# Local attention and a routed feed-forward layer on one core: row turns in steps apart, projection parts halved, layernorm and routing moved between GpSimd's folds, and the third routing table one block later

## The chip, the cores and the metric

The kernel runs on one core of one Trainium2 chip. The metric is the device time of one execution in microseconds (us). Five engines work side by side, each through its own instructions in the order in which the program gives them: TensorE (PE in the profile; its weight loads are PEld), VectorE (DVE), ScalarE (ACT), GpSimd (POOL) and SyncE (SP), which only issues DMAs. An instruction waits on semaphores for what it needs, and everything behind it on its engine waits with it.

## The reference

The input x is (2, 2048, 256) in f32. Two post-layernorm sublayers are computed:

```python
# causal local attention, 16 heads of 16, each row sees itself and the 64 before it
q, k, v = split(x @ W_attn + b_attn)
a = softmax(mask(q @ k.T / 4)) @ v
x1 = layernorm(x + a @ W_proj + b_proj)
# routed feed-forward: 8 experts, each token goes to the one with the largest logit
e = argmax(x1 @ Wr.T)
y = gelu(x1 @ W1[e] + b1[e]) @ Wo + bo + x1
out = layernorm(x1 + layernorm(y) * gamma + beta)
```

## The kernel before

**Attention loop.** The 4096 rows are 32 tiles of 128 and 8 chunks of 4 tiles. One loop of 32 steps handles four tiles at once, at different stages. In step i, tile t = i gets its scores (L513, L525, into four PSUM banks r = 0 to 3), its negated row maxima (`row_max`, L537, VectorE) and its exps (`exps`, L541, ScalarE, four per bank). GpSimd adds the exps up (`fold`, L553 after banks 0 and 1 and again after banks 2 and 3, then three halvings, L561). Tile u = i - 1 has its four banks of probabilities turned (`turn`, L591) and copied from PSUM (`keep_turned`: banks 0 and 2 by ScalarE, L597; 1 and 3 by VectorE, L599), and is weighed with v (`weigh`, L611). Tile w = i - 2 gets its sums inverted (`inverse`, L569, L574), spread by GpSimd (rw, L577), turned (`turn_inverse`, L630) and multiplied in (`normalise`, L634); then the output projection and the statistics for the layernorm (`join`, L642 to L652). Tile z = i - 3 gets the power of its variance on GpSimd (`norm_scale`, rs, L658 and L659), its layernorm x1 on VectorE (`norm`, L667) with a store of x1 to DRAM by SP (L670), and is turned for the router (`turn_x1`, L680; `keep_x1`, L685). Every fourth step computes router logits for four tiles (`route`, L692), turned one step later (`turn_logits`, L702).

**Projection parts.** Each chunk of x needs eight parts. Piece 0 turns the rows of x (`project`, L403, four short transposes per part); pieces 1 and 2 make q and k (L407, two 512-wide matmuls per part); piece 3 makes v (L414, four 256-wide matmuls per part). Each goes through a PSUM tile of a pool of two that `weigh` shares, and `keep` copies it out. A step has two slots for parts: slot 0 before the turns of banks 2 and 3, slot 1 behind them. Up to step 23 two parts run per step in plain order, so both parts of piece 0 fall into one step (3, 7, 11, and so on); steps 24 to 29 have one part each, in slot 1. `add_bias` (L1087, GpSimd) adds the bias to a chunk's residual at the end of a step.

**Routing.** Each token's expert, and its place among the tokens of that expert, is found by small VectorE operations, written as generators (`hot`, `places`, `first_blocks`, `other_blocks`, `rest_blocks`) that `some(task, n)` advances by n operations and `rest(task)` finishes. A dictionary `plan` gives them to the ends of steps. A table of the tokens of each block (`table`, L922) is a product of one-hot rows (`one_hots`, L827; `late_one_hots`, L833) and marks, accumulated by TensorE over all tiles. The first table is made in step 30; the second and third later.

**Blocks.** After the loop, 25 full blocks of 128 tokens of one expert each (`block(b)`) gather their tokens by an indirect DMA of GpSimd (L143), turn them (L181), run the first layer (L215) and the GELU (L226), and the second layer (L235); `finish_block` ends with two layernorms on VectorE and GpSimd (L245 to L265) and an indirect store (L267). The first layer of block b + 1 runs ahead of the second layer of block b. The remaining 7 x 128 tokens are taken in "late" blocks that the third table lists; 11 further first layers run over parts of these tokens, spread over the last full blocks (`firsts`), and seven second layers close the kernel. Dictionary `beside` gives the routing work to places (b, 0) to (b, 2) of the blocks; the third table stands at (13, 0), ahead of block 14's first layer, its rows in blocks 10 to 12 on VectorE (3 and 5 per block) and GpSimd (3, 3 and 2).

The order of every engine is the order of the calls: the whole is recorded under a manual schedule.

Of the kernel before, what the change touches and what calls it, by code (L numbers as in the profile page):

```python
# [33 lines left out]
def kernel(  # L34
# [90 lines left out]
    f6 = ctx.enter_context(tc.tile_pool(name="f6", bufs=5))  # L125
# [152 lines left out]
    with ExitStack() as att:  # L278
# [67 lines left out]
        off_i = aw.tile([P, P], I32, name="off_i")  # L346
        lag_i = aw.tile([P, 2, CTX], I32, name="lag_i")
# [50 lines left out]
        def project(c, piece, part):  # L398

            pm = psum(f"pj_{c}_{piece}_{part}")  # L400
            if piece == 0:
                for j in range(TPC):
                    nc.tensor.transpose(pm[:, ts(j, P)], xts[c][:, j, ts(part, P)], ident)  # L403
            elif piece in (1, 2):
                f = (piece - 1) * KC + part
                for k in range(KC):
                    nc.tensor.matmul(  # L407
                        pm, lhsT=wa[:, k, ts(f, P)], rhs=axT[c][:, k, :],
                        start=(k == 0), stop=(k == KC - 1),
                    )  # L410
            else:
                for a in range(2):
                    for k in range(KC):
                        nc.tensor.matmul(  # L414
                            pm[:, ts(a, C)],
                            lhsT=axT[c][:, k, ts(2 * part + a, P)],
                            rhs=wa[:, k, 2 * C : 3 * C],
                            start=(k == 0), stop=(k == KC - 1),
                        )
            pxs[c, piece, part] = pm  # L420

        def prepare(c, piece):

            first = c % (TPB // TPC) == 0
            if piece == 0:
                if c + 1 < B * T // CH:
                    xts[c + 1] = load_x(c + 1)
                axT[c] = p2.tile([P, KC, CH], F32, tag="xT", name=f"xT_{c}", bufs=1)
                xbs[c] = xp.tile([P, TPC, C], F32, tag="xb", name=f"xb_{c}")
            elif piece == 1:  # L430
                qs[c] = p2.tile([P, KC, 2, CH], F32, tag="q", name=f"q_{c}")
            elif piece == 2:
                ks[c] = p2.tile([P, KC, CTX + CH], F32, tag="k", name=f"k_{c}")
                if first:
                    nc.gpsimd.memset(ks[c][:, :, 0:CTX], 0.0)
                else:
                    nc.gpsimd.tensor_copy(ks[c][:, :, 0:CTX], ks[c - 1][:, :, CH : CH + CTX])
            else:

                vs[c] = p2.tile([P, TPC, NH // 2, 3, HD], F32, tag="v", name=f"v_{c}")  # L440
                nc.gpsimd.memset(vs[c][:, :, :, 1, :].rearrange("p j m d -> p (j m) d"), 0.0)

                vh[c] = p2.tile([P, TPC, NH // 2, 3, HD], F32, tag="h", name=f"h_{c}")
                if first:
                    nc.gpsimd.memset(vh[c][0:CTX, 0].rearrange("p m s d -> p (m s d)"), 0.0)

        def keep(c, piece, part):
# [31 lines left out]
            else:  # L479
                for a in range(2):  # L480
                    nc.vector.tensor_tensor(
                        vs[c][:, 2 * part + a, :, 0::2, :],
                        pm[:, ts(a, C)].rearrange("p (m s d) -> p m s d", s=2, d=HD),
                        bv_bc.rearrange("p (m s d) -> p m s d", s=2, d=HD),
                        ALU.add,
                    )
                v, h = vs[c], vh[c]
# [78 lines left out]
        def inverse(i):  # L566

            sm = small.tile([P, NH], F32, tag="sm", name=f"sm_{i}")
            nc.vector.tensor_reduce(sm, sums.pop(i)[:, :, 0:8], AX.X, ALU.add)  # L569
            spread_inverse(i, sm)  # L570

        def spread_inverse(i, sm):
            ri = small.tile([P, NH], F32, tag="ri", name=f"ri_{i}")
            nc.vector.reciprocal(ri, sm)  # L574
            rw = p2.tile([P, KC, 4, 2, HD], F32, tag="rw", name=f"rw_{i}")
# [86 lines left out]
        def norm(i):  # L662
# [3 lines left out]
            x1 = xp.tile([P, C], F32, tag="x1", name=f"x1_{i}", bufs=3)  # L666
# [20 lines left out]
        def route(c):  # L687
# [8 lines left out]
            lT = p2.tile([P, P], F32, tag="lT", name=f"lT_{c}")  # L696
# [19 lines left out]
        def iota(shape, pattern, base, cm, name):  # L716
            ti = rt.tile(shape, I32, name=f"{name}_i")
# [367 lines left out]
        def add_bias(c, tiles=TPC, first=0):  # L1085
            some = slice(first, first + tiles)
# [4 lines left out]

        for n in range(3):
# [7 lines left out]
        def quick_sums(i, r):  # L1100
# [4 lines left out]
            if r == 3:  # L1105
                spread_inverse(i, sums.pop(i))
# [3 lines left out]
        parts = [(c, n, p) for c in range(1, NT // TPC) for n in range(TPC) for p in range(2)]  # L1110
        work, at = {0: parts[:4]}, 4
        for i in range(1, NT - 2):
            count = 2 if i < NT - TPC - 4 else 1
            work[i] = parts[at : at + count]
            at += count
        assert at == len(parts)


        plan, spread, running = {}, {}, {}
# [15 lines left out]
        def put(at, *call):  # L1135
            plan.setdefault(at, []).append(partial(*call))


        for n, (t0, t1) in enumerate(lots[:EARLY]):
            at = t1 + 4  # L1140
            put(at, some, ("hot", n), 3)
            put(at + 1, rest, ("hot", n))
            put(at + 2, rank, n)
            put(at + 2, some, ("places", n), 1)
            put(at + 3, some, ("places", n), 3)
            put(at + 4, rest, ("places", n))
            for t in range(t0, t1, 2):
                spread[at + 5 + (t - t0) // 2] = [partial(one_hots, nc.gpsimd, t)]
        at = SPLIT[EARLY] + 6
        for n in range(7):  # L1150
            put(at + n, some, "first", 1 if n < 3 else 3)
        put(at + 7, rest, "first")
        put(at + 8, table, 0)
# [4 lines left out]
        for i in range(NT):  # L1158
# [3 lines left out]
            todo = work.get(i, [])  # L1162
            slots = [None] * (2 - len(todo)) + todo
            for part in todo:
                if part[2] == 0 and i > 0:
                    prepare(*part[:2])
# [4 lines left out]
            if i == 0:  # L1171
# [7 lines left out]
                for part in [(0, 3, 0), (0, 3, 1)] + todo[:2]:  # L1179
                    project(*part)  # L1180
                    keep(*part)
                add_bias(0)
                for r in range(2, 4):
                    exps(t, r)
                for part in todo[2:]:
# [7 lines left out]
            if u is not None:  # L1193
                turn(u, 0)
                keep_turned(u, 0)
                turn(u, 1)
            exps(t, 0)
# [3 lines left out]
            if z is not None:  # L1201
                norm_scale(z)
# [4 lines left out]
            row_max(t, 3)  # L1207
# [9 lines left out]
            if slots[0]:  # L1217
                keep(*slots[0])
            if z is not None:
                norm(z)  # L1220
            exps(t, 2)
            if slots[1]:
                project(*slots[1])
# [3 lines left out]
            if t == NT - 1:  # L1227
                for b in range(2):
                    gather(b)
                inverse(u)  # L1230
                quick_sums(t, 0)
            if slots[1]:
                keep(*slots[1])
# [23 lines left out]
            if i >= NT - TPC:  # L1257
                add_bias(i // TPC, 1, i % TPC)
            elif todo[-1:] and todo[-1][1:] == (3, 1):
                add_bias(todo[-1][0])  # L1260
# [84 lines left out]
    begin = 2 * NFULL - main + 1  # L1345
    for b in range(begin, NFULL):
        firsts[b].append(b - begin + NFULL)
    firsts[NFULL - 1].append(main - 1)
# [8 lines left out]
    def block(b):  # L1357
# [61 lines left out]
        (13, 0): [partial(table, 2)],  # L1419
# [5 lines left out]
    for b in range(10, 13):  # L1425
# [3 lines left out]
        beside[b, 2] = [partial(late_one_hots, nc.gpsimd, 3 * b - 6, min(3 * b - 3, NT))]  # L1429
# [76 lines left out]
```

## Time and profile before

| What | us |
|---|---|
| median of 3 runs (lowest, highest) | 604.82 (604.8, 605.92) |
| the profiled execution | 605.1 |
| its span, first to last instruction | 603.3 |
| first scores (step 0) start at | 14.86 |
| step 4 starts at | 51.83 |
| step 24 starts at | 245.08 |
| step 31 starts at | 311.54 |
| first second layer (block 0) starts at | 339.29 |
| second layer of block 12 starts at | 428.96 |
| last second layer (the 32nd) starts at | 585.56 |

The page divides the span into 40 slices of 15.1 us. Steps take from 8.0 to 12.6 us and full blocks 7.25 us where nothing else is in them, so two slices hold about three steps or four blocks. A matmul's end is modelled, so a busy TensorE in the profile is one with work in its pipeline. "ph", "py", "pj", "pt", "pa", "pr", "px", "pl" are PSUM tiles of the first layer, second layer or output projection, parts, turned probabilities, weighed values, turned inverse, turned x1 and logits.

### The profile page before, as it was taken

How to read it: one execution, taken by the hardware profiler on the slowest of the kernel's cores; microseconds unless marked ns; L12 is line 12 of the kernel's file. 1: busy time of each engine (PE TensorE's matmuls, PEld its weight loads, DVE VectorE, ACT ScalarE, POOL GpSimd, SP SyncE). 2: the span in 40 equal slices, each digit the busy share in tenths (PEclk: the TensorE clock that was granted, in tenths of full speed). 3: DMA queues.
4: the chain of work that ended last, by engine and by line, in shares of the span. 5: the costliest groups of instructions: out<-in, count | busy, mean ns of one | idle time of the engine just before them, and what ended most of it. 6: DMA issues, size and time to landing. Idle time of an engine off the chain costs nothing.

```text
span 603.3 us, 18546 instructions
## 1 busy us (share of the span) xinstructions
PE 560.2 (93%) x7311; PEld 455.8 (76%) x7312; DVE 406.6 (67%) x958; ACT 301.8 (50%) x1005; POOL 413.5 (69%) x613
## 2 busy tenths in 40 slices
PE   8999999999999999998978999999789999999990
PEld 5676766766767667666756898999689999999980
DVE  5668778789798788989976567887633323324482
ACT  2568666675657665675655433233224554554200
POOL 5367776776768868687873388888868766633473
PEclk9999999999999999999989999999989999999996
DMA  5311430210301202001423455555537677573010
GB/s 157 90 48 51 119 100 11 60 59 21 92 20 32 86 26 57 21 20 46 111 84 117 158 176 171 173 176 184 166 106 237 198 246 249 173 242 130 18 38 26
DMA packets 35605, 64.79 MB, mean 107 GB/s; under 512 B 8558, under 2 KB 23484, under 8 KB 35516
## 3 DMA queue, kind: packets, MB, share of 16 engines
q1 hardware_dynamic: 32444, 55.19, 29.3%
q0 software_dynamic: 3072, 8.39, 4.3%
q8 instruction: 59, 0.97, 0.7%
q14 instruction: 30, 0.25, 0.1%
HBM read 48.93 MB, written 8.39 MB: 95 GB/s over the span
## 4 chain that ended last, share of the span: by engine, by line
PE 66%; POOL 14%; DVE 9%; ACT 6%; issue 4%; DMA 0%; POOLq 0%; DVEq 0%; ACTq 0%
PE ph L215 14%; PE py L235 11%; PE pj L407 9%; PE pt L591 6%; PE pa L611 5%; PE s L525 5%; PE py L642 4%; PE pj L414 4%; ACT pr L541 4%; PE s L513 2%; POOL out_dram L267 2%; POOL xg L143 2%; DVE nm L537 2%; PE px L680 2%; POOL row L827 1%
## 5 line engine op out<-in xcount | busy, mean ns | idle before, releaser
L541 ACT ACTIVATE pr<-s,nm 128x128 f32<-128x128 f32 x512 | 140.9, 412 | 7.9 <-DVE nm L537 7.9
L553 POOL TENSOR_TENSOR fd<-pr 128x512 f32<-128x512 f32 x62 | 78.7, 1270 | 72.8 <-ACT pr L541 71.9
L226 ACT ACTIVATE gT<-ph,bc 128x128 f32<-128x128 f32 x200 | 57.0, 368 | 118.5 <-issue 63.0
L215 PE MATMUL ph<-xgT,wb 128*128 128x128 f32 x800 | 96.5, 279 | 0.0
L215 PEld LDWEIGHTS ph<-xgT,wb 128*128 128x128 f32 x800 | 95.3, 195 | 1.5 <-issue 0.2
L235 PE MATMUL py<-wo_sb,gT 128*128 128x256 f32 x400 | 90.6, 380 | 0.0
L537 DVE TENSOR_REDUCE nm<-s 128x4 f32<-128x512 f32 x128 | 81.6, 679 | 7.0 <-PE s L525 6.7
L561 POOL TENSOR_TENSOR fd<-fd 128x512 f32<-128x512 f32 (+2 forms) x93 | 76.4, 822 | 7.3
L235 PEld LDWEIGHTS py<-wo_sb,gT 128*128 128x128 f32 x400 | 74.1, 190 | 9.0
L597 ACT COPY pT<-pt 128x512 f32<-128x512 f32 x64 | 38.4, 601 | 82.6 <-DVE nm L537 27.9
L591 PE MATMUL pt<-ident,pr 128*128 128x128 f32 x512 | 71.8, 280 | 6.8 <-DVE pT L599 3.5
L591 PEld LDWEIGHTS pt<-ident,pr 128*128 128x128 f32 x512 | 55.9, 141 | 24.2 <-issue 10.6
L407 PE MATMUL pj<-xT,wa 128*128 128x512 f32 x128 | 60.1, 595 | 0.8 <-ACT xT L451 0.8
L255 DVE TENSOR_TENSOR y<-py,xbo 128x256 f32<-128x256 f32 x32 | 13.5, 422 | 57.7 <-PE py L235 54.3
L599 DVE COPY pT<-pt 128x512 f32<-128x512 f32 x64 | 43.7, 683 | 10.3 <-PE pt L591 10.2
L525 PEld LDWEIGHTS s<-k,q 32*64 32x64 f32 x2048 | 30.9, 130 | 13.6 <-issue 13.6
L215 PE MATMUL ph<-xpT,wb 128*128 128x128 f32 x352 | 40.9, 275 | 0.0
L215 PEld LDWEIGHTS ph<-xpT,wb 128*128 128x128 f32 x352 | 40.2, 192 | 0.1
L525 PE MATMUL s<-k,q 32*64 32x128 f32 x2048 | 38.6, 278 | 0.0
L642 PE MATMUL py<-wpj,av 128*128 128x256 f32 x128 | 34.2, 390 | 2.8 <-DVE logits L703 2.0
L265 DVE TENSOR_SCALAR res<-y,mv_c,rs_c 128x256 f32<-128x256 f32 x32 | 15.9, 498 | 30.5 <-POOL rs_c L249 30.4
L407 PEld LDWEIGHTS pj<-xT,wa 128*128 128x128 f32 x128 | 22.0, 190 | 18.9 <-issue 15.8
(236 smaller groups left out, 988.4 us busy)
## 6 DMA issues: line engine op xcount, KB each, us to landing
wb<-in_L_ffn_W_dram SPq DMA_DIRECT2D x33, 1024.0 KB, 5.2
h<-v SPq DMA_DIRECT2D x24, 192.0 KB, 3.8
xt<-in_L_attn_x_dram SPq DMA_DIRECT2D x8, 512.0 KB, 3.8
x_d<-x SPq DMA_DIRECT2D x32, 128.0 KB, 2.8
wb<-in_L_ffn_W_dram SPq DMA_DIRECT2D x24, 128.0 KB, 2.8
h<-v SPq DMA_DIRECT2D x14, 96.0 KB, 2.6
wo_sb<-in_L_ffn_Wo_dram SPq DMA_DIRECT2D x1, 1024.0 KB
wa<-in_L_attn_W_attn_dram SPq DMA_DIRECT2D x3, 256.0 KB, 5.8
```

The lines of the kernel that those rows point to most:

```text
L215: nc.tensor.matmul(phs[b, h][:, f % (NF // 2), :], lhsT=wb[:, k, ts(f, P)], rhs=xT[:, k, :], start=(k == 0), stop=(k == KC - 1),)
L226: nc.scalar.activation(gT[:, f, :], ph[:, f % (NF // 2), :], AF.Gelu, bias=bcs[b][:, f : f + 1], scale=1.0,)
L235: nc.tensor.matmul(py[:, 0:C], lhsT=gT[:, f, :], rhs=wo_sb[:, f, :], start=(f == 0), stop=(f == NF - 1),)
L407: nc.tensor.matmul(pm, lhsT=wa[:, k, ts(f, P)], rhs=axT[c][:, k, :], start=(k == 0), stop=(k == KC - 1),)
L525: nc.tensor.matmul(banks[i][r][a * CTX : (a + 1) * CTX, 2 * g + o, :], lhsT=qs[c][rows, g, o, t0 : t0 + CTX], rhs=ks[c][rows, g, t0 : t0 + P],
L537: nc.vector.tensor_reduce(maxes[i][:, r, :], banks[i][r], AX.X, ALU.max, negate=True)
L541: nc.scalar.activation(probs[i][:, r, x, :], banks[i][r][:, x, :], AF.Exp, bias=maxes[i][:, r, x : x + 1], scale=1.0,)
L553: nc.gpsimd.tensor_tensor(fd[:, 8 * pair : 8 * pair + 8, :], pr[:, two, :, 0:CTX].rearrange("p r x c -> p (r x) c"), pr[:, two, :, CTX:P]. ...
L561: nc.gpsimd.tensor_tensor(fd[:, :, 0:n], fd[:, :, 0:n], fd[:, :, n : 2 * n], ALU.add)
L591: nc.tensor.transpose(pt[:, x, :], probs[i][:, r, x, :], ident)
L599: nc.vector.tensor_copy(pTs[i][:, r], pt)
L642: nc.tensor.matmul(py[:, 0:C], lhsT=av[:, k, :], rhs=wpj[:, k, :], start=(k == 0), stop=(k == KC - 1),)
```

## The change

The work done stays the same except for its order; buffers change where the order needs it.

- Slots: `project` and `keep` take `halves`, so that a part may be done in two halves. The two turns of a chunk's rows now stand in slot 0 of two even steps, two steps apart (step 4m + 2 for chunk m + 2 and step 4m + 4), each with one whole matmul part in slot 1; odd steps have two whole matmul parts. From step 25 to 28, and in step 3, one part is halved over slots 0 and 1; the last part is halved over slot 1 of steps 29 and 30.
- In a step, GpSimd first makes rs (`norm_scale`), then rw (`spread_inverse`, split from `inverse`), then what `prepare` needs, then one half of `add_bias`, and only then the folds. `norm` moves up on VectorE, to behind the second copy of a turned bank and ahead of the row maxima of banks 2 and 3.
- Most routing operations move from the end of a step to behind `normalise` (`early`), those of the first table one step earlier at the end.
- Loads of x are issued with `add_bias` instead of with piece 0.
- Blocks: the third table moves to (14, 0); its rows are all made by VectorE in blocks 10 to 13. The 11 further first layers begin one block later (block 16) and the last two full blocks take two each.
- Buffers: xT 1 to 2, x1 3 to 2, lT 2 to 1, gathered tokens xg 5 to 4; some integer temporaries share other tiles.

```diff
-    f6 = ctx.enter_context(tc.tile_pool(name="f6", bufs=5))
+    f6 = ctx.enter_context(tc.tile_pool(name="f6", bufs=4))
...
-        def project(c, piece, part):
+        def project(c, piece, part, halves=(0, 1)):
-            pm = psum(f"pj_{c}_{piece}_{part}")
+            if (c, piece, part) not in pxs:
+                pxs[c, piece, part] = psum(f"pj_{c}_{piece}_{part}")
+            pm = pxs[c, piece, part]
...
-                for k in range(KC):
+                for k in halves:
...
-                if c + 1 < B * T // CH:
-                    xts[c + 1] = load_x(c + 1)
-                axT[c] = p2.tile([P, KC, CH], F32, tag="xT", name=f"xT_{c}", bufs=1)
-                xbs[c] = xp.tile([P, TPC, C], F32, tag="xb", name=f"xb_{c}")
+                axT[c] = p2.tile([P, KC, CH], F32, tag="xT", name=f"xT_{c}")
...
-            x1 = xp.tile([P, C], F32, tag="x1", name=f"x1_{i}", bufs=3)
+            x1 = xp.tile([P, C], F32, tag="x1", name=f"x1_{i}")
...
-        parts = [(c, n, p) for c in range(1, NT // TPC) for n in range(TPC) for p in range(2)]
-        work, at = {0: parts[:4]}, 4
-        for i in range(1, NT - 2):
-            count = 2 if i < NT - TPC - 4 else 1
-            work[i] = parts[at : at + count]
-            at += count
+        parts = [(c, n, p) for c in range(1, NT // TPC) for n in range(1, TPC) for p in range(2)]
+        line = iter(parts[2:])
...
+        work = {i: [None, None] for i in range(NT)}
+        for i in range(1, NT - 1):
+            c = i // TPC + (1 if i % TPC == 0 else 2)
+            if i % 2 == 0 and c < NT // TPC:
+                work[i] = [(c, 0, 0 if i % TPC else 1, (0, 1)), whole()]
+            elif i == 3 or NT - 7 <= i < NT - 3:
+                one = next(line)
+                work[i] = [one + ((0,),), one + ((1,),)]
+            elif i == NT - 3:
+                one = next(line)
+                work[i][1], work[i + 1][1] = one + ((0,), True), one + ((1,), True)
+            elif i < NT - 3:
+                work[i] = [whole(), whole()]
...
-        at = SPLIT[EARLY] + 6
-        for n in range(7):
-            put(at + n, some, "first", 1 if n < 3 else 3)
-        put(at + 7, rest, "first")
-        put(at + 8, table, 0)
+        at = SPLIT[EARLY] + 7
+        for n in range(6):
+            put(at + n, some, "first", 3 if n < 5 else 2, to=early)
+        put(at + 6, rest, "first", to=early)
+        put(at + 7, table, 0)
...
+            if z is not None:
+                norm_scale(z)
+            if w is not None:
+                spread_inverse(w)
...
+            if i >= TPC - 1 and i % TPC in (0, TPC - 1):
+                c = (i + 1) // TPC
+                if c < NT // TPC:
+                    add_bias(c, 2, 2 if i % TPC == 0 else 0)
+                if i % TPC == 0 and c + 2 < NT // TPC:
+                    xts[c + 2] = load_x(c + 2)
             exps(t, 0)
             row_max(t, 1)
             if u is not None:
                 keep_turned(u, 1)
             if z is not None:
-                norm_scale(z)
+                norm(z)
             if slots[0]:
                 project(*slots[0])
             exps(t, 1)
             row_max(t, 2)
-            row_max(t, 3)
+            if slots[0]:
+                row_max(t, 3)
             if t < NT - 1:
                 fold(t, 0)
...
-            if z is not None:
-                norm(z)
             exps(t, 2)
             if slots[1]:
-                project(*slots[1])
+                project(*slots[1][:4])
             if w is not None:
                 turn_inverse(w)
                 normalise(w)
...
+            for task in early.get(i, ()):
+                task()
...
-    begin = 2 * NFULL - main + 1
+    begin = 2 * NFULL - main + 2
...
-        (13, 0): [partial(table, 2)],
+        (14, 0): [partial(table, 2)],
...
-    for b in range(10, 13):
+    for b in range(10, 14):
         at = 8 * (b - 10)
         beside[b, 0] = [partial(late_one_hots, nc.vector, at, at + 3)]
         beside[b, 1] = [partial(late_one_hots, nc.vector, at + 3, at + 8)]
-        beside[b, 2] = [partial(late_one_hots, nc.gpsimd, 3 * b - 6, min(3 * b - 3, NT))]
```

## The prediction

> Steps of the attention loop are named by their number i; in steps 4 to 23 a chunk's eight projection parts repeat with i mod 4, so I call these steps S0, S1, S2, S3. Times are from the span's start.
>
> **What bounds the kernel now.** First the busy shares and the forty slices of the page.
>
> ```profile
> PE 560.2 (93%) x7311; PEld 455.8 (76%) x7312; DVE 406.6 (67%) x958; ACT 301.8 (50%) x1005; POOL 413.5 (69%) x613
> ...
> PE   8999999999999999998978999999789999999990
> DVE  5668778789798788989976567887633323324482
> ...
> POOL 5367776776768868687873388888868766633473
> PEclk9999999999999999999989999999989999999996
> ```
>
> TensorE is the bound nearly everywhere. Its work is the same after the change, so only its idle time, and time at a lower clock, can be won. It dips around slices 20 and 28 (about 300 and 430 us), where the clock dips too. The windows view, cut at the starts of steps (the first L513) and of second layers (L235), says how much each place holds.
>
> ```profile
> core 0: us, PE busy (x) PEld busy (x) DVE busy (x) ACT busy (x) POOL busy (x), PEclk, DMA share, GB/s
> ...
> 61.33:70.82 9.49, 9.49 (x165) 6.24 (x165) 6.79 (x14) 6.50 (x21) 6.35 (x10) 1.00 0.69 178
> 70.82:80.91 10.09, 10.09 (x190) 8.15 (x190) 7.73 (x19) 5.93 (x20) 7.58 (x11) 1.00 0.22 54
> 80.91:89.92 9.01, 7.75 (x170) 5.77 (x167) 7.02 (x14) 6.50 (x22) 6.90 (x9) 1.00 0.36 109
> ...
> 298.93:311.54 12.61, 9.24 (x191) 6.72 (x190) 9.24 (x20) 6.05 (x20) 8.80 (x12) 0.86 0.34 96
> ...
> 421.71:428.96 7.25, 7.25 (x53) 6.84 (x52) 4.92 (x13) 2.55 (x10) 6.13 (x11) 1.00 0.56 181
> 428.96:444.87 15.91, 11.05 (x85) 9.93 (x83) 9.05 (x27) 2.54 (x10) 13.58 (x22) 0.79 0.32 100
> 436.10:442.90 6.80, 4.00 (x22) 3.86 (x20) 3.83 (x12) 0.00 (x0) 5.72 (x9) 0.50 0.12 39
> ```
>
> A step with two matmul parts (61.33) holds no idle time; 70.82 has the routing matmuls besides. Step 7 with two row turns (80.91) idles 1.26. Step 30 (298.93) idles 3.4 and runs 3.4 us at half clock. A block is 7.25; the one with the third table takes 15.91. The timeline of step 7 shows why it idles:
>
> ```profile
> 82.46 2.37 POOL L1087 TENSOR_TENSOR xb<-xt,bp_bc 128x1024 f32<-128x1024 f32 x1
> ...
> 85.81 0.65 ACT L597 COPY pT<-pt 128x512 f32<-128x512 f32 x1
> 86.06 1.27 POOL L553 TENSOR_TENSOR fd<-pr 128x512 f32<-128x512 f32 x1
> 86.19 1.29 DVE L667 TENSOR_SCALAR x<-xb,mv,rs 128x256 f32<-128x256 f32 x1
> ...
> 86.60 0.41 PE L630 MATMUL pr<-ident,rw 128*128 128x128 f32 x2 [0.98 <-ACT pT L597]
> ```
>
> ScalarE copies the third turned tile only after eight exps, 5.6 us into the step; TensorE, with two 0.45 us turns instead of two 1.72 us parts, is there 1 us too early. TensorE's timeline of the long block:
>
> ```profile
> 433.93 0.18 PE L922 MATMUL p_tok<-marks,late_row 128*128 128x14 bf16 x1 [0.90 <-DVE late_row L833]
> ...
> 438.57 0.20 PE L922 MATMUL p_tok<-marks,late_row 128*128 128x14 bf16 x1 [2.42 <-POOL late_row L833]
> ...
> 439.25 5.56 PE L215 MATMUL ph<-xgT,wb 128*128 128x128 f32 x32
> ```
>
> The table waits for rows made on VectorE and, last, GpSimd; the first layer behind it runs partly at half clock: 5.56, against 3.73 in the block before.
>
> **Third table, a block later (blocks 13 and 14).** GpSimd loses eight rows (two groups of three at 1.91, one of two at 1.21: 5.0 us), VectorE gains eight in block 13. GpSimd's steps per block (L267 to L267) took 6.6 to 6.8 without rows and 8.3 with them, so with rows it fell behind TensorE's 7.25; without them it catches up. Do the rows come in time? In block 10 the fifth row of the second group ended at 419.19, 5.9 after the block's first L255 (413.28). That L255 lagged the second layer before it by 2.4, 1.8 in the next block; at 0.65 less per block it lags 0.5 at block 13, so the rows end 6.4 after a second layer whose successor ends at 7.25: slack 0.9. The table then costs 32 matmuls at 0.62/19, 1.05 us. Saving: 15.91 - 7.25 - 1.05 = **7.6**. If rows still come 1 to 2 us late and bring the clock down again, it is 4; bounds 3 to 8. Gather, turn and residuals of the late blocks move by a block with the table; their 10.6 to 11.0 us blocks are TensorE's alone, so order among them costs nothing, and weights keep over 10 us from a buffer's release to its use, against 5.2 to land (DMA part).
>
> A rule of the Trainium skill speaks against these rows: "SBUF — State Buffer", section "Who interferes with whom", has VectorE's tensor_scalar and GpSimd exclude each other for a whole instruction. The trace shows it: in block 10 three rows took 0.72 while GpSimd mostly issued a scatter, five took 2.24 beside its residuals, and a GpSimd power (L249) just after the three took 0.83 against 0.57. By the rule alone every row could stop GpSimd, 8 x 0.24 = 2 us, an estimate; the row above, a block of 6.6 with eight such rows, already contains what it costs.
>
> **Turns apart (steps 4 to 23).** Swapping a matmul part for a turn is worth 1.72 - 0.45 = 1.27 of TensorE. New steps without waits: S0 9.49 - 1.27 = 8.22, S1 9.49, S2 with routing 10.09 - 1.27 = 8.82, S3 9.49 + 0.27 for the logits = 9.76; sum 36.3. Steps 4 to 7 took 38.08 before (51.83 to 89.92), so 1.8 is at stake per period.
>
> But a wait is added: norm's L667 now stands on VectorE ahead of the third and fourth row maxima, and waits for GpSimd's rs. Queued behind it: both maxima, the fourth turned copy, hence exps 2 and 3 and the weighing. The chain from the last exps of a step: fold 1.27 and halvings 2.62 (with starts, 4.1), rs 0.19 + 0.55 + 0.1, x1 0.40, two maxima 1.28, turned copy 0.68: 7.3 to the weighing, and 2.2 from there to the next scores (68.62 to 70.82): 9.5. The exps end 7.6 into a step (76.27 + 2.17 - 70.82), or 8.3 with a q or k copy among them (98.21 - 89.92). So any two steps need 17.1 to 17.8, plus 0.64 where routing follows the weighing. S0+S1 has 17.7 of work: even. S1+S2 has 18.3, but the late maxima push S1's exps to 9.0: 9.0 + 9.5 + 0.64 = 19.1, so 0.1 to 0.9 is lost. x1 beside GpSimd's rw (0.40) or half bias (between 0.73 and 2.37, about 1.2) can lose 0.4 to 0.8 more in S0. The logits' wait of 0.28 stays. I take 1.25 of waits per period: 37.55, a gain of 0.53, times five: **2.7**. Bounds: nothing won (x1 meets a 1.27 fold as in 86.19), or all idle gone, 7.1 (the idle before TensorE in those steps).
>
> **Halves and early routing (steps 24 to 30).** They took 66.46 (245.08 to 311.54). TensorE has only 8.2 there, so the two-step chain sets them: (7.6 + 9.5)/2 = 8.55, about 8.6. Step 24 at 8.25, six at 8.6, plus two copies 0.7, routing twice 1.3, logits 0.5, table 0.5: 62.85, a gain of **3.6**. The halves fill the 0.28 that turns waited for a copy. The routing's last four operations (0.16, 1.30, 1.31, 0.82 from 297.85 on) delayed step 30's maxima; now two of them run a step earlier and all lie between the folds. If VectorE stays the limit (9.0 of 9.3 us busy in step 28) this gives 1; with all idle and the half clock gone, 8.5. The k copy for tile 28 now follows three small operations: at most 1 us late, inside these bounds.
>
> Clock: half clock followed waits of 0.56, 1.78 and 0.99 in step 30, and none followed the 0.98 in step 7. The Trainium skill ("TensorE: Matmul & The Clock Gate", section "What's actually happening") asks for an idle window of about 3.4 us. No single wait here was over 2.42, so the measurement decides: scattered waits suffice. By the rule these half-clock stretches would not be there to be won, about 3 us less gain.
>
> **At nothing.** Steps 0 to 3: the 0.98 wait of step 3 goes, the new chain takes as much: 0, between -0.7 and +1. Chunk 2's load goes out after the h copies, near 22.6 instead of 14.1, lands 3.8 later, is needed near 36. Later loads wait on SP for half a bias, with the x1 stores queued behind; with two x1 buffers a store has two steps, 18 us, for 2.8. Were that cover gone, L667 would stop VectorE, the same price as late rs. Gather buffers 5 to 4: the fifth was free a block early. Reordering before the blocks: 0, give or take 1.
>
> **Sum.** The profiled execution is 605.1 (span 603.3, 1.8 around it). 605.1 - 7.6 - 2.7 - 3.6 = 591.2. The median, 604.82, lies 0.3 lower: **590.9**.
>
> **Rivals.**
> - *The chain through rs eats the attention gain.* For: 9.5 plus 8.3 is already a period's work. Against: S3 and S0 have slack. Only the table remains, perhaps 1 us more: 596 to 598.
> - *Nearly all idle is filled.* For: two-part steps show 0.00 idle. It needs x1 never to wait: 604.8 - 7.6 - 7.1 - 8 = 582, up to 587.
> - *Slower.* L667 waits out a 1.27 fold after rs in every step, and the second maxima do again: 9.5 + 2.5 + 8.3 = 20.3 per two steps, 10.15 against 9.62 now (27 steps from 51.83 to 311.54). 27 x 0.53 = 14.3 lost, 7.6 won: 611. It decides from 9.90 per step on. Against: GpSimd's next fold waits for exps and now starts 0.8 after the rs before it or later (75.97, 95.07).
> - *The table still waits*, one block later, with the clock drop, and attention gives nothing: 601 to 604.
>
> **Chances.** Forecast (587 to 595) 0.52; chain eats it 0.22; all filled 0.17; table still waits 0.04; slower 0.05. Faster than 0.2% (1.2 us, what a measurement of this kernel can tell from none) 0.94, same 0.01 (the upper end of the fourth rival), slower 0.05. The range 583 to 598 holds the forecast, the first rival and most of the second; what is left out is under 0.2.
>
> **What would show it.** After: period about 37.5; step 7 without the L630 wait; S2's weighing (L611) waiting for the fourth turned copy or x1 for rs; step 30 below 10 us at full clock; L922 in one run of 32; blocks 12 and 13 at 7.25. Wrong if L667's idle time before it exceeds 1 us per step, or the table's waits reappear.

## The result, and the profile after

The changed kernel takes 607.34 us (median of 20 runs, 605.5 to 609.35), the kernel before 605.87 beside it (20 runs, 604.17 to 609.29): a ratio of 1.0015, 95% interval 1.0001 to 1.0029. It is level with the kernel before, or 0.1% slower, where 590.9 was forecast. The profiled execution after spans 604.95 us, 1.67 more than before. Cut at the same places as before:

| Stage | before | after | change | forecast |
|---|---|---|---|---|
| steps 0 to 3 | 36.97 | 36.53 | -0.4 | 0 |
| steps 4 to 23 | 193.25 | 203.31 | +10.1 | -2.7 |
| steps 24 to 30 | 66.45 | 65.64 | -0.8 | -3.6 |
| step 31 to the second layer of block 12 | 117.42 | 116.79 | -0.6 | 0 |
| from there to the last second layer | 156.60 | 148.83 | -7.8 | -7.6 |
| behind the last second layer's start | 17.72 | 19.02 | +1.3 | 0 |

One term came as forecast, and the attention loop gave all of it back. The page shows where TensorE lost what the blocks won: its busy share fell from 93% to 92%, and the loop's slices (1 to 21) now hold 8s, while the 7s and the low clock around slices 20 and 28 are gone.

```profile
PE 557.4 (92%) x7312; PEld 451.4 (75%) x7312; DVE 394.7 (65%) x966; ACT 303.2 (50%) x1005; POOL 409.8 (68%) x609
...
PE   8998998998989989989988899999999999999990
...
PEclk9999999999999999999999999999999999999996
```

The windows view after, cut at the starts of steps 10 (S2), 11 (S3), 12 (S0) and 13 (S1), then step 30 and blocks 12 and 13:

```profile
core 0: us, PE busy (x) PEld busy (x) DVE busy (x) ACT busy (x) POOL busy (x), PEclk, DMA share, GB/s
111.78:121.07 9.29, 9.06 (x182) 6.31 (x182) 7.42 (x16) 6.24 (x21) 6.21 (x9) 1.00 0.05 16
121.07:131.24 10.17, 9.89 (x177) 7.90 (x175) 7.26 (x17) 6.24 (x21) 9.03 (x12) 1.00 0.26 71
131.24:141.25 10.01, 8.67 (x165) 5.84 (x164) 7.92 (x18) 6.53 (x21) 5.39 (x9) 1.00 0.31 90
141.25:151.71 10.46, 9.57 (x167) 6.25 (x166) 7.86 (x17) 6.69 (x21) 7.18 (x11) 1.00 0.04 15
310.44:320.31 9.87, 8.69 (x194) 6.35 (x194) 7.13 (x18) 5.75 (x20) 7.22 (x10) 1.00 0.29 80
437.10:444.34 7.24, 7.24 (x52) 6.83 (x51) 5.90 (x17) 2.54 (x10) 6.10 (x9) 1.00 0.56 200
444.34:452.48 8.14, 8.14 (x85) 7.63 (x84) 6.70 (x20) 2.55 (x10) 6.78 (x11) 1.00 0.49 164
```

S2 and S3 stand where the prediction's terms put them (8.82 plus 0.1 to 0.9 lost, and 9.76 plus the 0.28 for the logits: 10.04). S0 takes 10.01 where 8.22 plus 0.4 to 0.8 was forecast, and S1 10.46 where 9.49 was; in both, busy time is well short of the length, at full clock. The four steps take 39.9 instead of 37.55. Step 30 and the two blocks came as forecast.

The timeline of S0 (step 12) names the wait. Columns are start, length, engine, line and operation, and in brackets the idle time before it and what ended it. Lines have moved by 4 to 7 against before: L407 turns rows, L411 makes q and k, L539 is the row maxima, L606 VectorE's copy of turned probabilities, L674 x1, L453 the copy of the second row turn.

```profile
133.84 0.60 PE L407 MATMUL pj<-ident,xt 128*128 128x128 f32 x4
134.72 0.54 DVE L674 TENSOR_SCALAR x<-xb,mv,rs 128x256 f32<-128x256 f32 x1
135.19 1.27 DVE L539 TENSOR_REDUCE nm<-s 128x4 f32<-128x512 f32 x2
135.35 1.02 PE L411 MATMUL pj<-xT,wa 128*128 128x512 f32 x2
136.39 0.68 DVE L606 COPY pT<-pt 128x512 f32<-128x512 f32 x1
136.98 0.68 DVE L453 COPY xT<-pj 128x512 f32<-128x512 f32 x1
137.71 1.12 PE L411 MATMUL pj<-xT,wa 128*128 128x512 f32 x2 [1.34 <-DVE xT L453]
```

In S0 the second turn of a chunk stands in slot 0 and the q part of the same chunk in slot 1. The q part's first product uses the turn of two steps ago, its second the turn of this very step. That turn is done at 134.4, but its copy stands on VectorE behind x1, two row maxima and the fourth turned copy, and lands at 137.66. TensorE waits 1.34 us, and has nothing else in its order to do.

In S1 (step 13) the same queue bites a second time:

```profile
145.56 0.60 DVE L674 TENSOR_SCALAR x<-xb,mv,rs 128x256 f32<-128x256 f32 x1 [0.73 <-POOL rs L666]
...
147.27 0.68 DVE L606 COPY pT<-pt 128x512 f32<-128x512 f32 x1
147.87 0.80 DVE L462 TENSOR_SCALAR q<-pj,bqkv,half 128x512 f32<-128x512 f32 x1
148.59 0.80 DVE L465 TENSOR_SCALAR q<-pj,bqkv,half 128x512 f32<-128x512 f32 x1
...
149.44 0.43 PE L618 MATMUL pa<-pT,h 128*32 128x64 f32 x16 [0.89 <-DVE q L465]
```

x1 waits 0.73 for rs, and what is behind it is that much later. The weighing (L618) does not read q: it needs a PSUM tile of the pool of two that it shares with the parts, and slot 0's tile is free only after both q copies, which stand last in VectorE's row.

The third table runs without a wait, ahead of block 15's first layer, which is at full clock (3.82 against 5.56):

```profile
444.34 3.62 PE L235 MATMUL py<-wo_sb,gT 128*128 128x256 f32 x16
447.80 0.95 PE L933 MATMUL p_tok<-marks,late_row 128*128 128x14 bf16 x32
448.60 3.82 PE L215 MATMUL ph<-xgT,wb 128*128 128x128 f32 x32
```

### The profile page after: what moved, and what is told of

Read it like the earlier page. It is cut to its first block, busy times and chain, and to the rows that moved or that the text cites. A ratio compares the mean times of both kernels' runs of the same rounds, so it can differ in the third digit from the quotient of the medians.

```text
span 604.9 us, 18523 instructions
## 1 busy us (share of the span) xinstructions
PE 557.4 (92%) x7312; PEld 451.4 (75%) x7312; DVE 394.7 (65%) x966; ACT 303.2 (50%) x1005; POOL 409.8 (68%) x609
## 4 chain that ended last, share of the span: by engine, by line
PE 56%; DVE 17%; POOL 11%; ACT 9%; issue 3%; DMA 2%; SPq 0%; POOLq 0%; DVEq 0%; ACTq 0%
PE ph L215 18%; PE py L235 15%; ACT pr L543 6%; DVE nm L539 5%; PE pj L411 4%; POOL fd L563 4%; PE py L649 3%; PE pj L418 3%; PE pa L618 3%; PE pt L598 3%; POOL fd L555 2%; PE s L527 2%; DVE pT L606 2%; POOL row L838 2%; DVE x L674 2%
## 5 line engine op out<-in xcount | busy, mean ns | idle before, releaser
L543 ACT ACTIVATE pr<-s,nm 128x128 f32<-128x128 f32 x512 | 142.5, 408 | 4.7 <-DVE nm L539 4.6
L215 PE MATMUL ph<-xgT,wb 128*128 128x128 f32 x800 | 94.7, 275 | 0.0
L215 PEld LDWEIGHTS ph<-xgT,wb 128*128 128x128 f32 x800 | 93.6, 192 | 1.5 <-issue 0.2
L539 DVE TENSOR_REDUCE nm<-s 128x4 f32<-128x512 f32 x128 | 82.3, 681 | 8.7 <-PE s L527 8.4
L411 PE MATMUL pj<-xT,wa 128*128 128x512 f32 x128 | 62.2, 600 | 9.1 <-DVE xT L453 8.3
L606 DVE COPY pT<-pt 128x512 f32<-128x512 f32 x64 | 43.5, 680 | 2.3 <-PE pt L598 2.2
L411 PEld LDWEIGHTS pj<-xT,wa 128*128 128x128 f32 x128 | 21.2, 190 | 27.8 <-DVE xT L453 14.0
L655 DVE TENSOR_TENSOR xb<-py,xb 128x256 f32<-128x256 f32 x32 | 13.6, 424 | 34.4 <-PE py L649 34.3
```

What stands on the lines that cost most here:

```text
L215: nc.tensor.matmul(phs[b, h][:, f % (NF // 2), :], lhsT=wb[:, k, ts(f, P)], rhs=xT[:, k, :], start=(k == 0), stop=(k == KC - 1),)
L411: nc.tensor.matmul(pm, lhsT=wa[:, k, ts(f, P)], rhs=axT[c][:, k, :], start=(k == 0), stop=(k == KC - 1),)
L539: nc.vector.tensor_reduce(maxes[i][:, r, :], banks[i][r], AX.X, ALU.max, negate=True)
L543: nc.scalar.activation(probs[i][:, r, x, :], banks[i][r][:, x, :], AF.Exp, bias=maxes[i][:, r, x : x + 1], scale=1.0,)
L606: nc.vector.tensor_copy(pTs[i][:, r], pt)
```

## The experiments

Two theories of the loss: A, it is S0's wait for a copy made in the same step; B, it is x1's new place on VectorE, ahead of the maxima. The stages named are those of the table above, from one profiled execution each; ratios are against the kernel before on the same chip.

**The late blocks alone.** The kernel before with the third table at (14, 0), its rows all on VectorE, the further first layers a block later; the attention loop as it was.

```diff
-    begin = 2 * NFULL - main + 1
+    begin = 2 * NFULL - main + 2
...
-        (13, 0): [partial(table, 2)],
+        (14, 0): [partial(table, 2)],
...
-    for b in range(10, 13):
+    for b in range(10, 14):
...
-        beside[b, 2] = [partial(late_one_hots, nc.gpsimd, 3 * b - 6, min(3 * b - 3, NT))]
```

> The kernel before with only the block part of the change (third table at block 14, its rows all on VectorE, late first layers a block later). Both theories put the whole loss of the change into the attention loop and agree here: from the second layer of block 12 to the last one 148.8 us as after the change, against 156.6 before, so 7.8 us faster than before, about 597 us in the profiled execution; the attention loop keeps its 193.3 us in steps 4 to 23. If this gains less than 6 us, the block part interacts with what comes before it and both are incomplete.

Measured: 598.32 us, ratio 0.9851 (0.9795 to 0.9907). From block 12's second layer to the last one 148.83, in every other stage the kernel before within 0.3. The block term is 7.8, needs nothing of the rest, and all of the loss but the 1.3 us behind the last second layer lies in the attention loop.

**The second turn one step after the first.** From the changed kernel, the second turn of a chunk moves from S0 to S3, so that no part reads a turn of its own step.

```diff
-            c = i // TPC + (1 if i % TPC == 0 else 2)
-            if i % 2 == 0 and c < NT // TPC:
-                work[i] = [(c, 0, 0 if i % TPC else 1, (0, 1)), whole()]
-            elif i == 3 or NT - 7 <= i < NT - 3:
+            c = i // TPC + 2
+            if i % TPC >= 2 and c < NT // TPC:
+                work[i] = [(c, 0, i % TPC - 2, (0, 1)), whole()]
+            elif NT - 8 <= i < NT - 3:
```

> The changed kernel with the second turn of a chunk's rows moved from S0 (where the q part behind it in the same step needs VectorE's copy of it) to S3, so that S2 and S3 hold one turn and one v part each and S0 and S1 two matmul parts. Theory A (the loss is the 1.34 us that TensorE waits in every S0 for that copy): the wait is gone, S0 about 9.6, S1 10.3 as now, S2 9.3, S3 8.9, a period of 38.1 against 39.8, 8 to 9 us less than the changed kernel: about 598. Theory B (the loss is x1's new place on VectorE, which makes every copy late): S0 becomes like S1, 10.3 with a wait of 0.7 for the q copy, S3 9.3, a period of 39.2: 3 us less, about 604.

Measured: 594.36 us, ratio 0.9778 (0.9721 to 0.9836); steps 4 to 23 192.69, so 10.6 less than in the changed kernel. S0 and S1 take 9.49 each. That is more than A asked for: S1's wait went as well. In step 13 rs is done 3.6 us into the step (142.07), against 4.3 in the changed kernel (145.52), and x1 does not wait for it any more.

**x1 back behind slot 0's copies.** From the changed kernel.

```diff
             if u is not None:
                 keep_turned(u, 1)
-            if z is not None:
-                norm(z)
...
             if slots[0] and slots[0][3][-1] == 1:
                 keep(*slots[0][:3])
+            if z is not None:
+                norm(z)
```

> The changed kernel with x1 (norm) back behind the copy of slot 0, where it was before the change; all else as changed. Theory A: the copy in S0 comes only 0.5 to 0.6 earlier, so 0.8 of the 1.34 us wait stays in S0; S1's 0.74 us wait for the q copy goes: a period of 38.5, 6 us less than the changed kernel, about 601. Theory B: both waits go (under 0.3 us each), a period of 37.7 or less: 10 us less or more, 597 or below.

Measured: 602.6 us, ratio 0.9921 (0.989 to 0.9953); steps 4 to 23 199.80, 3.5 less. S0 keeps 0.87 of its wait and S1 0.28 of its. The sums of TensorE's waits for these two from 120 to 245 us (total, times, longest) say it for the changed kernel first:

```profile
PE pj L411 <- DVE xT L453: 4.3, 3, 1.8
PE pa L618 <- DVE q L465: 2.4, 3, 0.9
```

and with x1 behind:

```profile
PE pj L411 <- DVE xT L453: 2.6, 3, 0.9
...
PE pa L618 <- DVE q L465: 0.9, 3, 0.3
```

x1's place feeds both waits but is not their root: A, with B as its smaller part. Over all five periods the two waits shrink from 10.4 us (7.0 in S0, 3.4 in S1) to 5.8, so by 4.6; the stage gained only 3.5 because a wait for the copied logits in step 15 grew from 0.91 to 2.32.

**Both.** The second turn in S3 and x1 behind the copies: the two edits above together.

> The changed kernel with both edits: the second turn in S3 and x1 back behind the copy of slot 0. Theory A: S0 9.5, S1 9.5, S2 9.0, S3 8.7, a period of 36.9, 14 us less than the changed kernel, about 593; the two edits add up. Theory B: as x1 back alone, about 597, since the turn's place then costs nothing either way.

Measured: 587.93 us, ratio 0.968 (0.9626 to 0.9735), better than both kernels and than either theory said. Steps 4 to 23 190.24, steps 24 to 30 61.38. In windows of steps 12 to 13 and 10 to 11 (S0, S1, S2, S3):

```profile
126.08:135.58 9.50, 9.50 (x166) 6.25 (x166) 8.39 (x19) 6.59 (x21) 7.11 (x9) 1.00 0.33 91
135.58:145.07 9.49, 9.49 (x165) 6.24 (x165) 7.26 (x17) 6.50 (x21) 6.28 (x10) 1.00 0.06 17
107.73:117.00 9.27, 9.06 (x185) 7.06 (x184) 8.04 (x17) 6.23 (x21) 6.37 (x10) 1.00 0.06 20
117.00:126.08 9.08, 8.80 (x173) 6.83 (x170) 6.86 (x16) 6.01 (x21) 7.45 (x11) 1.00 0.30 80
```

The period is 37.34. All that is left idle in these four is 0.21 in S2 and 0.28 in S3. The four kernels form a square for steps 4 to 23: moving the turn saves 10.6 (x1 ahead) or 9.6 (x1 behind), moving x1 saves 3.5 or 2.5.

**The copy first.** The changed kernel's order of parts, but in S0 the second turn and its copy come ahead of x1 and of the last maxima.

```diff
+            second_turn = slots[0] and slots[0][1:3] == (0, 1)
+            if second_turn:
+                project(*slots[0])
+                keep(*slots[0][:3])
             if z is not None:
                 norm(z)
-            if slots[0]:
+            if slots[0] and not second_turn:
                 project(*slots[0])
```

> The changed kernel, turns where the change put them (second turn in S0 with the q part behind it), but the second turn and VectorE's copy of it stand ahead of x1 and of the maxima of banks 2 and 3. Theory A (TensorE waits in S0 for that one copy): the copy ends near 4.3 us into S0 instead of 6.4, so the 1.34 us wait before the second half of the q part falls under 0.3 in each of six S0 steps; 0.68 later maxima give some of it back: 4 to 7 us less than the changed kernel, 600 to 603. Rival (S0 simply has too much queued on VectorE, whatever comes first): the wait moves to the weighing or to the next scores, and the time stays within 2 us of the changed kernel, 605 to 609.

Measured: 599.17 us, ratio 0.99 (0.9872 to 0.9928); steps 4 to 23 197.31. S0 falls to 8.58 in step 12, with no wait in it. But S1 now takes 10.70 (step 13), and the wait for q has grown from 2.4 to 3.2 over the same three periods:

```profile
PE pa L618 <- DVE q L465: 3.2, 3, 1.1
```

A shorter S0 leaves VectorE less time before S1, so part of the wait only moved. The copy is the cause of S0's wait; S1's needs VectorE's row to end earlier, or a matmul part in S0.

**The parts of the gain in steps 24 to 30.** Three undos, each from the best version, so that its 61.38 is the base. First the lone parts of steps 24 to 29 whole again, in slot 1:

```diff
-                one = next(line)
-                work[i] = [one + ((0,),), one + ((1,),)]
+                work[i] = [None, whole()]
...
-                one = next(line)
-                work[i][1], work[i + 1][1] = one + ((0,), True), one + ((1,), True)
+                work[i] = [None, whole()]
```

> Of the version with both edits (second turn in S3, x1 back; 587.9), the lone parts of steps 24 to 29 whole in slot 1 instead of halved over two places. If the halves are worth what they fill (0.28 of waiting for ScalarE's copy per step, and part of the wait for VectorE's copy), steps 24 to 30 lose 1.5 to 2.5 us: about 590. If the gain in these steps is all from the routing operations' new place, within 0.7 us of 587.9.

Measured: 589.31 us, ratio 0.9729 (0.9702 to 0.9757), steps 24 to 30 62.27. The halves are worth 0.9, between the two expectations. Second, the routing operations back at the ends of the steps, at their old step numbers:

```diff
-            put(at, some, ("hot", n), 3, to=early)
-            put(at + 1, rest, ("hot", n), to=early)
+            put(at, some, ("hot", n), 3)
+            put(at + 1, rest, ("hot", n))
...
-        at = SPLIT[EARLY] + 7
-        for n in range(6):
-            put(at + n, some, "first", 3 if n < 5 else 2, to=early)
-        put(at + 6, rest, "first", to=early)
-        put(at + 7, table, 0)
+        at = SPLIT[EARLY] + 6
+        for n in range(7):
+            put(at + n, some, "first", 1 if n < 3 else 3)
+        put(at + 7, rest, "first")
+        put(at + 8, table, 0)
```

> Of the version with both edits, the routing operations back at the ends of steps and at the old step numbers. If their place between the folds is what shortened steps 24 to 30 (61.4 us against 66.5 before the change), these lose 3 to 5 us, step 30 alone 2 or more: about 591 to 593. If the halves did it, within 1 us of 587.9.

Measured: 591.32 us, ratio 0.9756 (0.9731 to 0.9781), steps 24 to 30 64.34: the place of the routing is worth 3.0, 1.8 of it in step 30 (11.52 against 9.68), where the turned copy comes 1.78 late again. Of the last three operations before that table, VectorE's timeline shows, with the routing at the step's end:

```profile
293.64 0.31 DVE L910 TENSOR_TENSOR same<-label,at 128x144 f32<-128x144 f32 x1
293.98 1.43 DVE L917 TENSOR_TENSOR marks<-same,tile 128x144 bf16<-128x144 f32 x1
295.33 1.35 DVE L922 TENSOR_SCALAR marks<-same,own 128x144 bf16<-128x144 f32 x1
```

and in the best version, behind `normalise`:

```profile
283.32 0.31 DVE L910 TENSOR_TENSOR same<-label,at 128x144 f32<-128x144 f32 x1
...
291.43 0.30 DVE L917 TENSOR_TENSOR marks<-same,tile 128x144 bf16<-128x144 f32 x1
291.64 0.29 DVE L922 TENSOR_SCALAR marks<-same,own 128x144 bf16<-128x144 f32 x1
```

The same two operations take 1.43 and 1.35 while GpSimd folds, 0.30 and 0.29 between folds. Third, GpSimd's order as before (rw ahead of rs, rs behind the second turned copy, the whole bias at the end of S3):

```diff
-            if z is not None:
-                norm_scale(z)
             if w is not None:
                 spread_inverse(w)
...
-            if i >= TPC - 1 and i % TPC in (0, TPC - 1):
-                c = (i + 1) // TPC
-                if c < NT // TPC:
-                    add_bias(c, 2, 2 if i % TPC == 0 else 0)
-                if i % TPC == 0 and c + 2 < NT // TPC:
-                    xts[c + 2] = load_x(c + 2)
...
             if u is not None:
                 keep_turned(u, 1)
+            if z is not None:
+                norm_scale(z)
...
+            if i % TPC == TPC - 1 and i < NT - 1:
+                c = (i + 1) // TPC
+                add_bias(c)
+                if c + 2 < NT // TPC:
+                    xts[c + 2] = load_x(c + 2)
```

> Of the version with both edits, GpSimd's order as before the change: rw ahead of rs, rs behind the second turned copy, the bias of a chunk whole (2.4 us) at the end of S3. With x1 behind the copy of slot 0 the rs is needed only 6 us into a step, so by theory A this costs little: S0 at most 0.5 us each, 587.9 to 591. If GpSimd's order is what makes the new placement work, rw comes too late in S0 after the whole bias and TensorE waits there 1 us or more: 593 or above.

Measured: 589.58 us, ratio 0.9729 (0.9706 to 0.9752); steps 4 to 23 190.40, steps 24 to 30 62.49. GpSimd's new order is worth 1.1 in steps 24 to 30, and nothing before them.

**Both turns in one step again.** The best version with both turns of a chunk in S3.

```diff
-            if i % TPC >= 2 and c < NT // TPC:
-                work[i] = [(c, 0, i % TPC - 2, (0, 1)), whole()]
+            if i % TPC == 3 and c < NT // TPC:
+                work[i] = [(c, 0, p, (0, 1)) for p in range(2)]
```

> The best version so far (second turn in S3, x1 in its old place), with both turns of a chunk in one step again (S3, slots 0 and 1) and two whole matmul parts in S2. Steps 4 to 23 took 190.24 in that version and 193.25 in the kernel before. If the turns apart are what won there, S3 idles about 1 us again and steps 4 to 23 take 193 to 194: 591 to 592. If the rest of the change (GpSimd's order, early routing) won those 3.0, it stays at 588.

Measured: 592.7 us, ratio 0.9771 (0.9748 to 0.9794); steps 4 to 23 193.97, 3.7 more than in the best version, steps 0 to 3 36.89, 1.0 more. S3 idles 1.26 as before the change:

```profile
119.58:128.59 9.01, 7.75 (x170) 5.78 (x167) 7.03 (x14) 6.49 (x22) 5.81 (x9) 1.00 0.24 70
```

**The turns apart alone.** The version with the late blocks alone, and in it only the parts' order: first turn in S2, second in S3, each in slot 0 (with a second xT buffer, and the change's smaller buffers to make room).

```diff
+        for i in range(3, NT - TPC - 4, TPC):
+            work[i - 1][1], work[i][0] = work[i][0], work[i - 1][1]
+            work[i - 1].reverse()
+            work[i].reverse()
```

> The version with the late blocks' change alone (598.3, steps 4 to 23 in 193.32, steps 24 to 30 in 66.52), plus only the turns apart (first turn in S2, second in S3, each in slot 0 with a part of v in slot 1; two xT buffers and the memory for them). If the turns apart need nothing else, steps 4 to 23 take about 190.3 and the kernel 595.3; if they need GpSimd's new order or the early routing, 597 to 599. Steps 24 to 30 stay at 66 to 67 by both.

Measured: 612.48 us, ratio 1.011 (1.0065 to 1.0155): slower, which neither case had. Steps 4 to 23 take 207.23, and the loss sits in S0 (and, at half clock, in the step behind it). Step 8:

```profile
88.90:102.85 13.95, 10.76 (x166) 6.72 (x166) 9.34 (x17) 6.63 (x21) 10.94 (x13) 0.94 0.43 125
```

The timelines of step 8, of SP's queue, of VectorE and of TensorE, one after the other (L285 loads x, L671 stores x1, L668 makes x1, L681 turns it):

```profile
93.83 0.38 SPq L285 DMA_DIRECT2D xt<-in_L_attn_x_dram  x1
94.30 0.46 SPq L671 DMA_DIRECT2D x_d<-x  x1
...
96.73 0.55 SPq L671 DMA_DIRECT2D x_d<-x  x1
```

```profile
98.62 1.39 DVE L668 TENSOR_SCALAR x<-xb,mv,rs 128x256 f32<-128x256 f32 x1 [2.65 <-POOL fd L554]
```

```profile
100.16 0.41 PE L681 MATMUL px<-ident,x 128*128 128x128 f32 x2 [2.94 <-DVE x L668]
```

In the kernel before, a load of x is issued with piece 0. In this order that is S2, while its buffer comes free only with the bias at the end of S3 (93.80). SP's queue stood still for the load, with two stores of x1 behind it, and x1 has two buffers: it waits for a store to leave. In step 8 the profile writes the wait down to a GpSimd fold because that was the last event it saw; rs itself was done at 94.91. In steps 12, 16 and 20 it names the store (total, times, longest):

```profile
DVE x L668 <- DMA x_d<-x: 8.6, 3, 3.3
```

**The same with the loads behind the bias**, as the change has them.

```diff
-                if c + 1 < B * T // CH:
-                    xts[c + 1] = load_x(c + 1)
...
                 add_bias(todo[-1][0])
+                if todo[-1][0] + 2 < NT // TPC:
+                    xts[todo[-1][0] + 2] = load_x(todo[-1][0] + 2)
```

> The version before it (late blocks plus turns apart alone) lost 2.9 us in S0, where x1 waited for a store of x1 that stood on SP's queue behind a load of x, which waited for the residual's bias. Here each load of x is issued right after that bias, as in the change. If that queue was the whole loss, S0 takes about 9.5, steps 4 to 23 about 190.4, and the kernel 595 to 596. If the turns apart also need GpSimd's new order or the early routing, steps 4 to 23 take 192 or more: 597 to 600.

Measured: 596.6 us, ratio 0.9854 (0.983 to 0.9878). Steps 4 to 23 take 190.58 against 193.32 with the late blocks alone, steps 0 to 3 35.86 against 36.97: 3.8 gained by the turns apart, with nothing else of the change but the loads' place. Steps 24 to 30 took 68.51 against 66.52: 1.2 more in step 30, which ran longer at half clock (0.75 against 0.86 in the mean), and 0.8 more in step 24. So the two versions' whole times can't be told apart.

## Why the prediction was wrong, step by step

**The late blocks: right.** 7.8 against 7.6; the rows came in time, and L933 runs in one piece.

**The turns apart: the step that failed.** "New steps without waits: S0 9.49 - 1.27 = 8.22" took the input of the part in S0's slot 1 as ready. It is the copy of the turn in slot 0 of the same step. The list "Queued behind it: both maxima, the fourth turned copy" left out the next entry of VectorE's row, `keep(slot 0)`: the copy of xT in S0, the two q copies in S1. So S0 lost 1.20 to 1.76 in every period, and S1 0.74 to 0.89 in four and 0.28 in the fifth: 10.4 us together in steps 4 to 23, of the 15.6 that TensorE idles there (7.1 before). The diff had said it: `work[i] = [(c, 0, 0 if i % TPC else 1, (0, 1)), whole()]`, with c the chunk whose q part is the next in the line.

A second step was mis-sized: "1.8 is at stake per period". The rows shown with it held the right figure. The four busy times of before are 9.49, 9.49, 10.09 and 7.75, 36.8 together, not 36.3; with 0.27 for logits, a turn in place of a part saved (9.49 + 0.27 - 7.75)/2 = 1.0, not 1.27. At stake was the 1.26 of idle in S3.

With the dependency taken away the term was about right: 2.7 was forecast for steps 4 to 23, and the turns apart gave 2.7 alone and 3.7 in the best version. That it came so near is partly luck: the work of a period was put 0.5 too low (36.3 for 36.8), and its waits 0.8 too high (1.25 for the 0.5 of the best version).

**Halves, early routing and GpSimd's order: mechanism right, size low.** Steps 24 to 30 gained 5.1 in the best version against 3.6 forecast (routing's place 3.0, GpSimd's order 1.1, halves 0.9 by the undos). In the changed kernel they gained 0.8. There step 24, which still has the second turn and a q part, takes 11.38 (8.30 in the best version), with waits of 1.17 and 1.30, and the table's step 30 came as forecast: 9.87, at full clock.

**At nothing.** Steps 0 to 3 gave 1.1 where step 3's wait went and no new one came (best version). The cover named for the loads held in the changed kernel; the run with the turns alone shows its price where it is gone, 207.23 - 190.58 = 16.7 us over steps 4 to 23: four waits of 1.79 to 2.99 for x1, 10.7 together, and behind three of them 13.7 us at half clock. The last stores lost 1.3 in the changed kernel and in the one with x1 back, in none of the others; the store before the last begins 1.8 us after its input is there (591.55 to 593.34), against 0.3 in the kernel before. Why is open.

**The rivals.** In number "The table still waits" (601 to 604) and "Slower" (611) lie nearest to 607.34, but neither by its mechanism: the table ran without a wait, and L667 (now L674) did not wait out a fold in every step, 0.75 was its longest wait in steps 4 to 23. "The chain through rs" had its place, x1 ahead of the maxima, as 2.5 to 3.5 of the loss (4.6 by the two waits alone). None named a part's own input, and so neither of the two signs set for "wrong" appeared, though the forecast was wrong.

**Shared ports, and the clock.** The Trainium skill ("SBUF — State Buffer", section "Who interferes with whom") says that one of VectorE and GpSimd blocks the other for a whole instruction where both want the ports that they share. The trace agrees: 1.43 and 1.35 beside folds of 1.27, 0.30 and 0.29 without. For the late rows the block time settled it: block 12, with rows in it, takes 7.24.

The Trainium skill ("TensorE: Matmul & The Clock Gate", section "What's actually happening") asks for an idle window of about 3.4 us, and calls that window free-running. The traces show such a window, but it need not be all idle. In the 13 profiled executions all changes of the granted clock lie on one grid of 3.41 us per execution. Half clock followed each window of that grid in which TensorE idled 2.03 us or more, one of two with 1.90, and none with less (the ends of matmuls are modelled, so the hundredths are rough). Around the wait of 2.94 with the turns alone, at 97.22 to 100.16:

```profile
97.84:101.25 3.41, 0.83 (x4) 0.56 (x5) 2.63 (x4) 0.37 (x1) 3.17 (x5) 1.00 0.96 261
101.26:104.67 3.41, 3.41 (x40) 1.74 (x47) 2.11 (x7) 0.00 (x0) 0.20 (x2) 0.50 0.04 10
104.68:108.08 3.40, 3.40 (x61) 2.22 (x46) 2.72 (x5) 1.99 (x7) 1.07 (x3) 1.00 0.00 0
```

The waits of 1.34 and 1.76 in S0 of the changed kernel stayed under the limit, at full clock. So the prediction had it right that scattered waits suffice, and what counts is their sum within a window. The same order of work in step 30, with waits of 0.55 to 0.57, 1.77 to 1.78 and 0.99, ran at 0.87 with the turns alone and at 0.75 with the loads moved too: the grid cut its idle time into 2.47 and 0.30 in the first, which gave one window at half clock, and into 2.03 and 0.73 in the second, which gave two (in the 13 traces half clock ended after a window with up to 0.58 of idle time, and went on after one with 0.73 or more).

## What to carry to other kernels

When a schedule moves a piece of work, write down for each moved piece which copy its input comes from and in which slot that copy stands on the other engine; a producer and its consumer in the same step are only as close as the queue between them. Check the sum of a period's busy time against the profile before calling idle time from it. When a step pays less than its idle time, look also at what shares its buffers: a pool of two made the weighing wait for copies that it never reads, and one load issued early held the stores, and through two buffers the layernorm, for up to three microseconds.

## What the runs showed that was not expected

- A load that waits on SP's queue cost more than any compute edit here, 16.7 us: waits of TensorE of 1.79 to 2.99 in four of five periods, one of which the profile names as a wait for a GpSimd fold.
- Half clock followed waits of 0.55, 1.78 and 0.99 in one step 30 and not waits of 0.43, 1.78 and 0.55 in another (routing back): 0.86 to 0.87 against 1.00. In the second, no 3.41 us window of the clock held more than 1.78 of idle time.
- In the best version TensorE is busy for 554.8 us, 95% of a span of 585.7. Of the rest, 14.1 us lie behind its last matmul, and from step 0 on no single wait is longer than 0.97.
